# Self attention of a decoder kernel: input scalings over two turns, weights prepared differently, another order on VectorE

## The chip, the cores and the metric

The kernel runs on one core of a Trainium2 chip. A core has five engines that run at the same time, each with its own queue: TensorE (PE) for matmuls and transposes, VectorE (DVE), ScalarE (ACT), GpSimd (POOL), and SyncE (SP), which here only issues DMA transfers. The metric is the device time of one execution in microseconds (us); lower is better. Beside the timed runs there is one profiled execution, from which all durations of single instructions come.

## The reference, cut to what matters

Two decoder layers are computed on x of shape 16 x 112 x 512. The part that the change touches is the first layer's second attention. It has a self part (q, k, v from the normalised x) and a cross part (queries from x, keys and values from a context of 375 rows); the two results go through one output projection together.

```python
def _div_clamp_fp8(x, scale):
    y = jnp.clip(x.astype(jnp.float32) / scale, -FP8_MAX, FP8_MAX)
    return _fp8_roundtrip(y.astype(jnp.bfloat16).astype(jnp.float32))
def _fp8_linear_pertensor(x, wq, w_scale, in_scale):
    xq = _div_clamp_fp8(x, in_scale)
    return jnp.einsum('bsi,oi->bso', xq * in_scale, wq) * w_scale
...
ln_out = _ln(hidden_states, ln_w, ln_b)
q = _ln(_fp8_linear_pertensor(ln_out, wq, wq_scale, q_in_scale).reshape(b, s, g, hpg, d), qln_w, qln_b)
k = _ln(_fp8_linear_pertensor(ln_out, wk, wk_scale, k_in_scale).reshape(b, s, g, d), kln_w, kln_b)
v = _fp8_linear_pertensor(ln_out, wv, wv_scale, v_in_scale).reshape(b, s, g, d)
core = _gqa(q, k, v).reshape(b, s, nh * d)
...
catq = _div_clamp_fp8(jnp.concatenate([core, xout], axis=-1), proj_smooth)
return jnp.einsum('bsi,oi->bso', catq, wproj) * (proj_in_scale * proj_w_scale)
```

So the input is scaled in four ways (for q, k, v and for the cross queries) and rounded to an 8-bit float; the projections are normalised per head; 16 heads share 8 groups of keys; and a scalar, proj_in_scale times proj_w_scale, multiplies the output.

## The kernel before

The program runs in stages; the one concerned is `stage_fp8_self`, from about 286 to 950 us of the profiled span. The 1792 tokens form 14 tiles of 128, the heads four quarters of four. The stage has 64 units of work, each one quarter q and one batch b. Two batches in sixteen (b = 7 and 15) have no tile of their own and do less. The order of units is fixed by `self_order`: eight units of quarter 0, then units of quarters 0 and 1 mixed until unit 24, the rest of quarter 1 to unit 31, quarter 2 from 32 to 47, quarter 3 from 48 to 63.

The loop body is `turn(n)`, which works on several units at once: it projects unit n, computes scores and exponentials of unit n-2, transposes probabilities and multiplies values of unit n-3, transposes queries and keys of unit n-1, and adds the output of unit n-4. The order in which the steps stand in `turn` is the order of instructions on PE and ScalarE for the whole loop, and on VectorE too from turn 5 on (`manual_schedule`). GpSimd's and SP's orders, and VectorE's before turn 5, are set by a planner when the program is built.

What happens in a turn, by engine, with the lines of the profile:

- PE: `ps_q` (L664), scores `ps_s` (L826), transposed probabilities `ps_pt` (L850), `ps_kv` (L664, keys then values), `ps_av` (L858), transposed queries and keys `ps_t` (L819), output `ps_acc` (L664). In some turns also the transposes of an input tile, `ps_xt` (L154). In turns -2 to 4 there are early products for the cross stage, `ps_early` (L653). Weights are in two parts, high and low, so each projection is two products.
- ScalarE: squares of the queries (L761), copy of the probabilities (L852), four exponentials (L839), squares of the keys (L761), copy of the values (L792), queries and keys into batches, `qt` and `kt` (L485).
- VectorE: minimum of the scores, `su_m` (L832), sums of squares, `su_v` (L764), reciprocal (L843), smoothing and rounding of the values (L883, then L504 to L508), normalisation, `qk` (L804), addition to x (L899).
- GpSimd: the last subtraction of a rounding (L510), probabilities times reciprocal (L844), the power of -1/2 for the normalisation (L491 and L492).

The normalisation L804 frees the PSUM banks of `ps_q` and `ps_kv`; there are three banks for the two tiles of each turn.

Three further jobs are woven in. The first is the inputs (`Quantized`). While quarter 0 runs, an input tile is transposed, scaled by 16 ScalarE instructions of one 128x128 block each (L695), rounded on VectorE and GpSimd (`round_qk` for q and k, `round_v` for v; both call `round_fp8`), and written to DRAM for later quarters. Turn n does all of it for unit n+2: the transposes and five scalings around the exponentials, five more and `round_qk` after the key and value products, six more and `round_v` at the end. Inputs come in turns -2 to 4, 6, 8, 10, 13, 15, 17 and 20.

The second is the weights of the next quarter (`Weights`). A piece of 512 columns is loaded in one of two buffers (`begin`), centred on VectorE if it belongs to queries or keys (`centers`: mean L587, L593, subtraction L594), and split into its high part on ScalarE (L617) and its low part on GpSimd (L618) (`ends`). Value and output weights are scaled on ScalarE (L616) ahead of the split. In `turn`, `ends` stands first, `begin` in the middle, `centers` near the end. Quarter 1's weights come two pieces a turn from turn 3, quarter 2's two a turn from turn 24, quarter 3's one a turn from 31, the first cross weights one a turn from 47. The first self weights are prepared in the stage before, the further cross weights in the stage behind, by `step`.

The third is `quantize_cross`: it loads a scaled input tile from DRAM, rounds it for the cross queries and stores it, one of 14 tiles at the end of each turn n in which unit n-4 is of quarter 2 and has a tile.

## Time and profile before

| what | value |
|---|---|
| median of 3 runs | 3885.63 us (3881.12 to 3893.52) |
| the profiled execution, its own time | 3916.36 us |
| its span, first to last instruction | 3914.6 us |
| mean granted TensorE clock | 0.969 |
| PE busy | 3647.7 us (93%) |
| VectorE busy | 1758.7 us (45%) |
| ScalarE busy | 1464.3 us (37%) |
| GpSimd busy | 938.1 us (24%) |

Busy time is a union over an engine's instructions; shares are of the span. The shares are means over seven stages with different limits, so a stage is read by itself. A line of the timeline has the start, the duration, the engine, the line of the program, the operation, output<-inputs and shapes, how many are merged (x8) and, in brackets, how long the engine had been idle and what ended that. "128x512" is partitions by elements. The granted clock is what the throttle gave TensorE[...].

### The profile page before, as it was taken

Reading aid. Unit: us, or ns where it says so; the run is one execution under the profiler, and the core shown is the slowest. Engines: PE = TensorE matmul, PEld = TensorE weight load, DVE = VectorE, ACT = ScalarE, POOL = GpSimd, SP = SyncE. Lnnn points to the kernel's source line nnn. Section 1 sums busy time; section 2 is a strip of 40 time slices with the busy share of each in tenths; the row PEclk is TensorE's granted clock in tenths of the full one; section 3 lists DMA queues with packets and bytes.
Section 4 is the critical chain, followed back from the end, with each engine's and each line's share of the span. In section 5 each row is a group of like instructions: output and inputs, shape, how many; then the busy total and the mean of one; then the engine's idle time right before and its main releaser. Section 6 shows DMA issues by size and latency. Waiting matters only on the chain.

```text
span 3914.6 us, 46312 instructions
## 1 busy us (share of the span) xinstructions
PE 3647.7 (93%) x16482; PEld 2350.9 (60%) x16482; DVE 1758.7 (45%) x3856; ACT 1464.3 (37%) x4189; POOL 938.1 (24%) x1322
## 2 busy tenths in 40 slices
PE   7888788989899999999999999998889989999999
PEld 4445678877556666566666554554344445556788
DVE  4446767775554544544445551111233343214333
ACT  2546666654544444444444430110123341112222
POOL 2333545553322322322222210000222220000000
PEclk8999889999999999999999999999999999999999
DMA  2125323442211211211121115999930013122000
GB/s 74 56 96 171 113 85 117 135 133 75 75 51 60 74 47 48 68 50 51 44 82 48 40 65 180 314 291 260 290 109 12 1 38 111 63 79 81 11 12 17
DMA packets 118117, 364.56 MB, mean 93 GB/s; under 512 B 13280, under 2 KB 33248, under 8 KB 108848
## 3 DMA queue, kind: packets, MB, share of 16 engines
q1 hardware_dynamic: 105504, 332.20, 26.8%
q0 software_dynamic: 5040, 16.52, 1.3%
q10 hardware_dynamic: 7344, 12.89, 1.0%
q8 instruction: 131, 2.15, 0.2%
q14 instruction: 98, 0.80, 0.1%
HBM read 317.09 MB, written 44.47 MB: 92 GB/s over the span
## 4 chain that ended last, share of the span: by engine, by line
PE 68%; DVE 8%; DMA 6%; ACT 3%; POOL 3%; issue 3%; SPq 0%; ACTq 0%; POOLq 0%; DVEq 0%
PE ps_kv L1081 14%; PE ps_acc L664 4%; PE ps L1430 4%; PE ps_q L664 4%; PE ps_av L1134 4%; DMA w_expert<-in_moe_w 3%; PE ps_s L1109 3%; PE ps_u L1785 3%; PE ps_o L341 3%; PE ps_o L1767 3%; PE ps_g L1785 3%; PE ps_q L1536 3%; PE ps_p L1629 3%; PE ps_pt L1124 2%; PE ps_y L1448 2%
## 5 line engine op out<-in xcount | busy, mean ns | idle before, releaser
L1081 PE MATMUL ps_kv<-w_kv,ct 128*125 128x512 f32 x1408 | 637.4, 592 | 0.0
L1081 PEld LDWEIGHTS ps_kv<-w_kv,ct 128*125 128x125 f32 x1408 | 261.1, 187 | 277.2 <-issue 242.1
L1430 PE MATMUL ps<-w_expert,xgt 128*128 128x448 f32 x560 | 222.1, 549 | 19.8 <-DMA w_expert<-in_moe_w 19.1
L510 POOL TENSOR_TENSOR r_o<-r_t,r_m 128x64 fp32r<-128x64 bf16 (+6 forms) x224 | 146.9, 674 | 390.6 <-DVE r_t L508 366.1
L1025 ACT ACTIVATE pr<-ps_s,ex_m 112x375 f32<-112x375 f32 (+1 forms) x272 | 157.7, 580 | 161.6 <-DVE ex_m L1024 151.5
L1057 DVE TENSOR_REDUCE cu_v<-sq 125x2 f32<-125x256 f32 (+1 forms) x248 | 118.5, 478 | 179.3 <-ACT sq L1056 179.0
L233 POOL TENSOR_TENSOR pr<-pr,nq_s 112x448 f32<-112x448 f32 (+1 forms) x120 | 119.5, 996 | 323.7 <-DVE nq_s L232 248.9
L492 POOL TENSOR_TENSOR cu_v<-cu_v,mhalf 125x2 f32<-125x2 f32 (+1 forms) x248 | 190.3, 767 | 20.7
L228 ACT ACTIVATE pr<-ps_s,nq_m 112x112 f32<-112x112 f32 (+1 forms) x480 | 167.7, 374 | 59.0 <-DVE nq_m L220 54.6
L491 POOL TENSOR_SCALAR cu_v<-cu_v 125x2 f32<-125x2 f32 (+1 forms) x248 | 48.2, 194 | 577.9 <-DVE cu_v L1057 575.0
L1109 PE MATMUL ps_s<-kt,qt 128*112 128x375 f32 x512 | 183.0, 479 | 1.3 <-ACT pr L1025 0.9
L1024 DVE TENSOR_REDUCE ex_m<-ps_s 112x1 f32<-112x375 f32 (+1 forms) x272 | 148.4, 545 | 71.8 <-PE ps_s L1656 68.2
L1430 PEld LDWEIGHTS ps<-w_expert,xgt 128*128 128x128 f32 x560 | 104.3, 192 | 117.5 <-issue 107.1
L1056 ACT ACTIVATE sq<-ps_kv 125x256 f32<-125x256 f32 x176 | 67.6, 384 | 273.0 <-PE ps_kv L1081 220.9
L485 ACT ACTIVATE qt<-ps_t,turned 128x448 f32<-128x448 f32 (+6 forms) x224 | 116.6, 582 | 137.6 <-PE ps_t L1093 126.6
L1134 PE MATMUL ps_av<-pt,vn 125*128 125x224 f32 x768 | 161.4, 360 | 0.0
L1124 PEld LDWEIGHTS ps_pt<-ident,pr 112*125 112x125 f32 x768 | 103.5, 190 | 88.6 <-DVE pr L1116 49.9
L242 ACT COPY ptt<-ps_pt 112x448 f32<-112x448 f32 (+1 forms) x120 | 67.4, 561 | 226.3 <-PE ps_pt L240 226.2
L1109 PEld LDWEIGHTS ps_s<-kt,qt 128*112 128x112 f32 x512 | 90.1, 177 | 99.8 <-issue 60.2
L1134 PEld LDWEIGHTS ps_av<-pt,vn 125*128 125x128 f32 x768 | 144.6, 193 | 8.5 <-ACT pt L1127 4.0
L1124 PE MATMUL ps_pt<-ident,pr 112*125 112x112 f32 x768 | 119.0, 286 | 31.5 <-DVE pr L1116 30.5
L485 ACT ACTIVATE kt<-ps_t,vec 128x375 f32<-128x375 f32 (+7 forms) x240 | 131.6, 589 | 26.5 <-PE ps_t L1099 22.3
(294 smaller groups left out, 7426.4 us busy)
## 6 DMA issues: line engine op xcount, KB each, us to landing
w_expert<-in_moe_w SPq DMA_DIRECT2D x105, 896.0 KB
ct<-in_ctx_t SPq DMA_DIRECT2D x64, 750.0 KB
xq<-xq_dram SPq DMA_DIRECT2D x42, 512.0 KB
xq<-xx_dram SPq DMA_DIRECT2D x56, 256.0 KB
raw<-in_self_w SPq DMA_DIRECT2D x48, 256.0 KB
w_sum<-in_ffn_w SPq DMA_DIRECT2D x12, 1024.0 KB
cn<-in_ctx SPq DMA_DIRECT2D x16, 750.0 KB
xv<-xv_dram SPq DMA_DIRECT2D x48, 224.0 KB
```

The lines of the kernel that those rows point to most:

```text
L228: nc.scalar.activation(pr[:, j, :], self.ps[:, j, r * t : (r + 1) * t], AF.Exp, bias=self.mx[r][:, j : j + 1], scale=-1.0, accum_out=sums[ ...
L485: k.nc.scalar.activation(dst, src, AF.Identity, bias=cols[:, 1:2], scale=cols[:, 0:1])
L492: nc.gpsimd.tensor_tensor(dst, dst, bc(k.minus_half[: dst.shape[0]], [dst.shape[0], n]), ALU.pow)
L664: k.nc.tensor.matmul(out, lhs(c), w[i][:, c, :], start=first and c == 0 and i == 0, stop=last and c == n - 1 and i == 1,)
L1024: nc.vector.tensor_reduce(mx, src, AX.X, ALU.min)
L1025: nc.scalar.activation(dst, src, AF.Exp, bias=mx, scale=-1.0, accum_out=sums)
L1081: nc.tensor.matmul(pkv, self.ct[:, c, ch * CC : (ch + 1) * CC], w[:, c, :], start=c == 0, stop=c == KC - 1,)
L1109: nc.tensor.matmul(ps, self.heads.qt[self.b][:, h, :], self.kt[:, h // 2, :], start=True, stop=True)
L1124: nc.tensor.transpose(ps[:, h, :], self.pr[:, h, ch * CC : (ch + 1) * CC], k.ident[:S, :S])
L1134: nc.tensor.matmul(av[:, 2 * g : 2 * g + 2, :], self.vn[:, ch, g, :], self.pt[:, ch, 2 * g : 2 * g + 2, :], start=ch == 0, stop=ch == NCH - 1,
L1430: nc.tensor.matmul(pp, self.xt[:, c, :], w[:, c, :], start=c == 0, stop=c == 3)
L1785: nc.tensor.matmul(pp, w[:, c, cols], xt[:, part, c, :], start=c == 0 and part == 0, stop=c == 3 and part == 1,)
```

## The change

- **Inputs.** Turn n now takes the transposes and the first ten scalings of unit n+2, near its end, and, for unit n+1, `round_qk` behind the query sums, the last six scalings behind the exponentials and `round_v` behind the normalisation.
- **Weights in a turn.** `centers` now treats the pieces loaded in the turn before, behind the minimum, the query sums and `round_qk`; `ends` follows in the same turn behind the exponentials. `centers` also returns whether it centred anything.
- **Output weights.** They are no longer scaled. The scalar `c_proj` is applied when the output is added to x, by one instruction with a scale (L905 in place of L899), in the cross stage too.
- **Value weights.** ScalarE writes the scaled high part at once (two instructions of 256 columns), and the low part is one VectorE instruction for each half (L620: raw times scale less the high part) instead of GpSimd's subtraction.
- **Output of unit n-4.** It comes behind the new input's transposes.
- **Cross roundings.** One tile is taken in every turn from 32 on in which nothing was centred, behind the normalisation, until the 14 are done.

```diff
     def centers(self):
-        for center, end in self.loaded:
-            if center:
-                center()
-            if end:
-                self.begun.append(end)
+        centers = [center for center, _ in self.loaded if center]
+        for center in centers:
+            center()
+        self.begun += [end for _, end in self.loaded if end]
         self.loaded = []
+        return len(centers) > 0
...
         def end():
             hi, lo = self.hi[n][:, cols], self.lo[n][:, cols]
-            if not centered:
-                for i in rows:
-                    part = raw[:, i * width - first : (i + 1) * width - first]
-                    nc.scalar.activation(part, part, AF.Copy, scale=col(i))
-            nc.scalar.copy(hi, raw)
-            nc.gpsimd.tensor_tensor(lo, raw, hi.bitcast(F32), ALU.subtract)
+            if centered or scale is None:
+                nc.scalar.copy(hi, raw)
+                nc.gpsimd.tensor_tensor(lo, raw, hi.bitcast(F32), ALU.subtract)
+                return
+            for i in rows:
+                part = slice(i * width - first, (i + 1) * width - first)
+                nc.scalar.activation(hi[:, part], raw[:, part], AF.Copy, scale=col(i))
+                nc.vector.scalar_tensor_tensor(
+                    lo[:, part], raw[:, part], col(i), hi[:, part].bitcast(F32),
+                    ALU.mult, ALU.subtract,
+                )
...
-    k.nc.vector.tensor_tensor(k.x[:, t, :], k.x[:, t, :], acc, ALU.add)
+    x = k.x[:, t, :]
+    k.nc.vector.scalar_tensor_tensor(x, acc, k.c_proj, x, ALU.mult, ALU.add)
...
         def turn(n):
-            new = inputs.get(n + 2)
-            for w in weights:
-                w.ends()
+            new, half = inputs.get(n + 2), inputs.get(n + 1)
             products(early.get(n, 0))
             if at(n):
                 units[n].project_q(weights[order[n][0]], xq.pop(n))
@@
             if at(n):
                 units[n].query_sums()
-            if new:
-                new.transpose()
+            if half:
+                half.round_qk()
+                xq[n + 1] = half.xq
+            centered = [w.centers() for w in weights]
             if at(n - 3):
                 units[n - 3].transpose_probs()
             if at(n - 2):
                 units[n - 2].exponentials()
-            if new:
-                new.scale(5)
+            for w in weights:
+                w.ends()
+            if half:
+                half.scale(6)
             if at(n):
                 units[n].project_kv(xv[order[n][0]].pop(order[n][1]))
             for w, count, pieces in due(n):
                 w.begin(count, pieces)
-            if new:
-                new.scale(5)
-                new.round_qk()
             if at(n - 3):
                 units[n - 3].values()
             if at(n):
                 units[n].normalize()
+            if half:
+                half.round_v()
+            if n > last[1] and tiles and not any(centered):
+                quantize_cross(k, wk, tiles.pop(0))
             if at(n - 1):
                 units[n - 1].transpose()
-            if at(n - 4):
-                units[n - 4].output()
             if new:
-                new.scale(6)
-                new.round_v()
-                xq[n + 2] = new.xq
+                new.transpose()
+                new.scale(10)
             elif at(n + 2):
                 q, b = order[n + 2]
                 xq[n + 2] = quantized(k, wk, b, xv[q]) if q else None
+            if at(n - 4):
+                units[n - 4].output()
...
-            for w in weights:
-                w.centers()
-            if at(n - 4) and order[n - 4][0] == 2 and units[n - 4].tile is not None:
-                quantize_cross(k, wk, units[n - 4].tile)
```

More of the change, by code (lines that the diff above doesn't have):

```diff
@@ L603, in part @@
         k.raw_load = nc.sync.dma_start(out=raw, in_=src[:, cols])
-        col = lambda i: k.c_proj if scale is None else k.w_cols[:, scale + i : scale + i + 1]
+        col = lambda i: k.w_cols[:, scale + i : scale + i + 1]
         rows = range(first // width, (first + 512) // width)
@@ L954, in due @@
                     yield weights[q + 2], 2 if q == 0 else 1, 3 if n >= last[q] + 4 else 1 + (q < 2)
+        tiles = list(range(TILES))
         def turn(n):
-            new = inputs.get(n + 2)
-            for w in weights:
-                w.ends()
+            new, half = inputs.get(n + 2), inputs.get(n + 1)
             products(early.get(n, 0))
```

## The prediction

> **What bounds the kernel now.** Read first: busy time by stretches. The change sits in the self attention stage (286 to about 950 us of the span): 64 turns, one per pair of quarter and batch, numbered 0 to 63. The first row is turns 5 to 9, then 10 to 24, 25 to 31, 32 to 47, 48 to 63, and last the eight turns 56 to 63 alone.
>
> ```profile
> 389.00:443.60 54.60, 38.59 (x204) 33.09 (x204) 39.82 (x75) 37.62 (x109) 34.05 (x35) 0.81 0.36 121
> 443.60:593.40 149.80, 128.94 (x776) 114.39 (x776) 100.33 (x218) 94.62 (x312) 73.56 (x89) 0.91 0.28 91
> 593.40:657.00 63.60, 55.06 (x352) 48.93 (x350) 46.92 (x104) 41.02 (x126) 38.73 (x42) 0.97 0.39 125
> 657.00:794.00 137.00, 127.54 (x808) 113.10 (x806) 103.55 (x241) 80.87 (x264) 79.01 (x93) 0.96 0.42 137
> 794.00:929.20 135.20, 125.29 (x807) 111.83 (x805) 98.16 (x229) 78.08 (x256) 70.40 (x86) 0.97 0.34 109
> 868.90:929.20 60.30, 60.30 (x406) 54.77 (x403) 39.27 (x92) 37.29 (x124) 29.47 (x38) 1.00 0.28 89
> ```
>
> Columns: stretch, its us, busy PE, PE loads, DVE, ACT, POOL, granted clock, DMA. The last row is the stage undisturbed: PE busy all the time at clock 1.00, 60.3 us for eight turns, 7.54 us each. By that measure turns 5 to 63 need 59 x 7.54 = 444.6 us, and 3.0 for seven input transposes (0.43 each); the distance between the first value products of turns 4 and 63 in the timeline (374.2 and 929.2) is 555. So 107 us of this stage are lost, 2.7% of the kernel. That is all the change can win, but for crumbs elsewhere.
>
> Second, who PE waited for in 316 to 930 us (total, times, longest):
>
> ```profile
> PE ps_av L858 <- ACT pt L852: 27.5, 15, 5.4
> PE ps_kv L664 <- DVE qk L804: 19.3, 10, 4.0
> PE ps_s L826 <- ACT kt L485: 10.1, 7, 3.9
> PE ps_acc L664 <- ACT pr L839: 8.0, 3, 3.0
> ```
>
> These make 65 of some 71 us of idle time; the other 36 of the 107 are matmuls at a reduced clock.
>
> Third, the timeline of one turn with a bad wait (turn 11, kv product at 465.65). VectorE, then PE and ScalarE:
>
> ```profile
> 459.49 0.43 DVE L504 TENSOR_SCALAR y<-y 128x1024 bf16<-128x1024 bf16 x1 [0.90 <-ACT y L695]
> ...
> 460.87 0.69 DVE L508 TENSOR_TENSOR r_t<-y,r_m 128x1024 bf16<-128x1024 bf16 x1
> ...
> 462.13 1.82 DVE L504 TENSOR_SCALAR r_y<-r_y 128x448 bf16<-128x448 bf16 x1
> ...
> 464.92 0.68 DVE L804 TENSOR_TENSOR qk<-ps_q,su_v 128x512 f32<-128x512 f32 x1
> ...
> 467.76 0.62 DVE L832 TENSOR_REDUCE su_m<-ps_s 112x4 f32<-112x448 f32 x1
> ```
> ```profile
> 465.65 1.19 PE L664 MATMUL ps_kv<-w_self,xq 128*128 128x256 f32 x8 [2.68 <-DVE qk L804]
> ```
> ```profile
> 468.47 0.36 ACT L839 ACTIVATE pr<-ps_s,su_m 112x112 f32<-112x112 f32 x1 [3.70 <-DVE su_m L832]
> ```
>
> Ten of the 16 scalings must run on ScalarE before VectorE may round (459.49); the smoothing behind it is held by GpSimd's xq subtraction (1.82 us instead of 0.28); only then comes normalisation, which frees the PSUM bank for which PE waits; and the minimum, whose scores PE had at 462.6, comes at 467.76. Weight turns have the same shape: two centrings stand before the minimum, and the second is stretched:
>
> ```profile
> 599.78 0.75 DVE L594 SCALAR_TENSOR_TENSOR raw<-raw,w_cols,w_mean 128x512 f32<-128x512 f32 x1
> ...
> 601.42 1.68 DVE L594 SCALAR_TENSOR_TENSOR raw<-raw,w_cols,w_mean 128x512 f32<-128x512 f32 x1
> 603.03 0.61 DVE L832 TENSOR_REDUCE su_m<-ps_s 112x4 f32<-112x448 f32 x1
> ```
>
> **The change, part by part.** Step sizes are start-to-start from these timelines. A turn's fixed VectorE work is 5.1 us: minimum 0.54, query sums 0.60, reciprocal 0.15, key sums 0.34, smoothing 1.95, normalisation 0.94, addition to x 0.59. Rounding q and k is 2.0, rounding v 1.3, centring a 512-wide piece 1.65 (two: 3.3), four 256-wide groups 4.5.
>
> *1. Inputs spread (ten scalings at the end of turn n, six in n+1, q/k rounding at the start of n+1).* The count is the same. A turn on ScalarE without scalings is 5.3 us; 16 more at 0.37 make 11.2 against 8.6 of PE, so now one turn overflows and its neighbour idles. Spread: 9.0 and 7.5. Rounding q/k no longer waits for ScalarE in its turn and falls where VectorE waits for the exponentials (1.0 to 1.5 us a turn). Its deadline is one turn nearer: xq is ready about 5 us before its product. The moved DMAs (xq, yx, xv stores) keep their count; on SP the loads queued behind them are wanted two turns later, and the weight load, which waits there for its buffer's last subtraction, now has until the middle of the next turn. The output product moves behind the input's transposes on PE; no engine waits for either at once.
> Turns 5 to 9: VectorE after needs 5.1+3.3+2.0+1.3 = 11.7, then 9.6 (5.1+4.5), 8.4 (no query in turn 7: 3.2, roundings 3.3, two value pieces 1.9), 5.1 and 8.4; with a wait of about 1 us in the long ones, and PE's 8.6 elsewhere, 12.7+10.6+9.4+8.6+8.9 = 50, against 69.3: **-19**. Turns 10 to 24: clean 15 x 7.54 + 2.2 = 115.3; the five turns with roundings are 8.4 of VectorE plus waits, 1.2 above clean each, and 4 for what I do not see: 125 against 149.8: **-25**.
>
> *2. Minimum first, centring behind it, copies after the exponentials.* The exponentials come 3.3 us sooner in two-piece turns. But in the new order the squares of the keys stand on ScalarE behind the weight copies, and those behind the centring of the same turn; GpSimd's order puts a weight subtraction (1.29) ahead of the power for normalisation. Minimum to normalisation then takes about 10 us in two-piece turns against 11.7 (their mean now is 63.6/7 = 9.1 over all kinds). Turns 25 to 31: **-4**. Turns 32 to 63 centre one piece a turn, which fits PE's 8.2; they lose 16.4 and 14.6 now (137.0 and 135.2 less 120.6).
>
> *3. Cross roundings in turns without centring.* Now they meet centrings in turns 48 to 52 (key weights 4.1 us plus rounding 1.4 before the minimum). After, each with its load and its store on SP, ten fall in turns 38 to 47 and four in 53 to 56; VectorE 5.1+1.4 plus waits still fits 8.2, not the short turns of 5.3. With the one-piece centrings of step 2 I count half the 31 us as won: **-15**.
>
> *4. Lighter weights.* Output weights lose their ScalarE scaling (0.73 x 4 a set), value weights a copy and GpSimd's subtraction (2 x 0.62, 2 x 1.29 a set), and VectorE gets four fused subtractions a set. No row shows that form; nearest is the 256-wide L594, 0.48. Floor 0.4, ceiling 0.48 plus a GpSimd xq operation of 2.1 in the way: I take 0.48, so 1.9 a set, counted in turn 7 above. In the first attention and the cross stage (PE busy 1293 of 1330 us) it is behind PE: 0 to -4, take **-1**.
>
> *5. Addition with scale.* The like form is L1802, xo from ps_o with a scalar and x, 128x512: mean 745 ns against 682 for L899. 112 x 0.063 = 7 us of VectorE, mostly under PE; in cross PE waits for VectorE 28.7 us, so at most 3.5 there. Take **+2**, bounds 0 and +7.
>
> *The clock.* [...] Here a wait of 2.74 us (turn 14) is followed by kv matmuls at 2.08 us for eight instead of 1.17; one of 2.68 (turn 11) by 1.19. [...] By the rows nearly all 36 hang on these waits. [...]
>
> Sum: -19 -25 -4 -15 -1 +2 = -62 us. Steps 1 to 3 (63) assume the planned overlap; each engine has its order fixed and each handover (0.2 to 1 us in the waits) delays the next, so I keep three quarters: 63 x 0.75 = 47, less 1 net for 4 and 5: **-46**. The profiled execution took 3916.4 us (span 3914.6) and would take 3870. It is 0.8% above the median of the runs, 3885.6; nothing says that this surplus is in the changed stage, so the same 46 us off the median give **3840 us**.
>
> **Rivals.**
> A, *VectorE stays the bound* (0.15): the work is the same, 5.1 plus up to 6.6 in a turn, and GpSimd's subtractions still stretch two-input operations (0.75 to 1.68 above), now the centring behind the q/k rounding. For it: VectorE busy 39.8 of 54.6 us in turns 5 to 9. Against: half its loss is waits for ScalarE. If only a quarter of steps 1 to 3 is won: 3870.
> B, *all of it is won and the clock stays up* (0.10): 80 to 100 of the 107 us, 3795.
> C, *slower* (0.12): the squares of the keys. They now stand behind six scalings (2.2 us) or the weight copies (1.2, and the centring they wait for), so key sums, power and normalisation come later, and PE's next kv product waits for the bank. From the end of one kv product to the start of the next is 6.3 us; the chain needs 3.0, plus 2.2 fits, plus copies and centring does not. 24 turns have scalings or centring. It decides from 2.6 us of new wait in each, which eats the 62; at 3.4 us, with the half-speed matmuls behind such waits, 82 - 62 = +20: 3905.
> D, *nothing moves* (0.06): another wait of the same length appears (scores for kt, which ScalarE writes last): 3886.
>
> **The numbers.** My case has 0.57 and by itself runs from 3815 to 3862. Within 0.3% (12 us), which is about what a measurement of this kernel tells from no change, is D and a quarter of A (0.04), which runs from 3862 to 3883; the rest of A, my case and B are faster: faster 0.78, same 0.10, slower 0.12. Low is 3802 (B's nearer end), high 3883 (A's far end); C, most of D and the deeper half of B are left out.
>
> **What would show it.** Right: the stretch of the stage shorter by 40 to 60 us, turns 10 to 24 near 8.4 us each, clock there above 0.95, VectorE's waits for ScalarE's y gone, the smoothing near 0.3, PE's waits for qk under 5 us. Wrong: new waits of PE for qk or kt, of VectorE for the key squares, or a centring that waits for its weights' DMA, which is now loaded a turn ahead.

## The result, and the profile after

The changed kernel takes 3876.15 us (median of nine runs, 3872.43 to 3882.13); the kernel before takes 3885.63 in nine runs of its own (3879.88 to 3893.52). The ratio is 0.9978, with a 95% interval of 0.9968 to 0.9988. That is 9.5 us less where 46 were forecast: the sign was right, the size a fifth, and the 0.22% of the ratio lies within the 0.3% that the prediction took for no change.

The profiled execution took 3873.2 us of span against 3914.6, which looks like 41 us; most of it is not the change. The first product of the cross stage stands at 950.9 us of the span before and at 941.7 after, 9.2 us earlier, about the gain of the medians. The other 32 us come after the changed stage. The section on the hardware returns to them.

For the stage, the busy time by stretches of the changed kernel: turns 5 to 9, 10 to 24, 25 to 31, 32 to 47, 48 to 63, and turns 56 to 63 alone. A turn ends where its first value product begins. Columns: stretch, its us, busy PE, PE loads, DVE, ACT, POOL, granted clock, DMA share, GB/s.

```profile
382.30:444.10 61.80, 46.23 (x254) 40.18 (x254) 48.08 (x96) 43.35 (x134) 35.37 (x39) 0.86 0.35 111
444.10:575.50 131.40, 120.40 (x777) 106.21 (x777) 98.83 (x222) 97.55 (x320) 75.33 (x90) 0.99 0.34 113
575.50:640.70 65.20, 56.94 (x352) 50.05 (x350) 50.23 (x103) 37.64 (x120) 33.77 (x38) 0.95 0.37 116
640.70:782.40 141.70, 126.62 (x807) 110.73 (x805) 106.73 (x246) 77.91 (x258) 77.90 (x92) 0.99 0.42 133
782.40:919.90 137.50, 126.60 (x808) 111.97 (x806) 102.17 (x233) 75.78 (x252) 72.23 (x88) 0.98 0.34 109
859.60:919.90 60.30, 59.60 (x385) 53.67 (x385) 43.54 (x98) 34.87 (x115) 31.87 (x40) 0.97 0.31 99
```

The first row that the prediction shows of before (389.00 to 443.60, 54.6 us) leaves out turn 5 and is turns 6 to 9 alone. The prediction's sums use the right 69.3. The row of before to compare with is:

```profile
374.20:443.60 69.40, 47.47 (x251) 40.86 (x250) 47.48 (x95) 47.34 (x140) 40.74 (x43) 0.80 0.36 120
```

Turns 5 to 9 and 10 to 24 became shorter by 7.6 and 18.4 us. Turns 25 to 31 and 32 to 63 became longer, by 1.6 and 7.0. One stretch that the prediction did not sum at all also became longer: from the first early product to the first value product of turn 4 the stage took 87.2 us before and takes 94.7. The balance, -26.0 + 8.6 + 7.5, is -9.9 us.

What PE waits for in 307 to 920 us of the changed kernel (total, times, longest):

```profile
PE ps_s L831 <- ACT kt L485: 17.0, 10, 4.2
PE ps_kv L669 <- DVE qk L809: 11.9, 11, 3.7
PE ps_acc L669 <- ACT pr L844: 9.6, 6, 1.7
PE ps_kv L669 <- POOL xv L510: 8.0, 6, 1.9
PE ps_xt L154 <- ACT y L700: 4.8, 5, 2.2
PE ps_t L824 <- DVE x L905: 4.2, 4, 2.1
...
PE ps_av L863 <- ACT pt L857: 2.1, 3, 1.1
```

The greatest wait of before, 27.5 us for the copied probabilities, has all but gone, and the wait for `qk` fell from 19.3 to 11.9. But `kt` grew from 10.1 to 17.0, and rows that before lacked in this stretch have come: `xv` (8.0), the input's `y` (4.8), the addition to x (4.2).

In the turn that the prediction took apart, the change does what it was to do. VectorE in turn 11 of the changed kernel:

```profile
460.59 0.30 DVE L504 TENSOR_SCALAR r_y<-r_y 128x448 bf16<-128x448 bf16 x1
...
465.19 0.62 DVE L837 TENSOR_REDUCE su_m<-ps_s 112x4 f32<-112x448 f32 x1 [1.31 <-PE ps_s L831]
...
466.35 0.42 DVE L504 TENSOR_SCALAR y<-y 128x1024 bf16<-128x1024 bf16 x1
```

The minimum waits for nothing but its scores, the rounding follows at once without a wait for ScalarE, and the smoothing's first step takes 0.30 us instead of 1.82. Turn 11 took 11.7 us before and takes 8.7. But its neighbours now carry the rest of the same work, and turns 10 to 12 together took 32.3 us before and take 32.4. The gain of 18.4 us lies in turns 14 to 24, above all in 14, 16, 18 and 22. The question is what was lost elsewhere.

### The profile page after: what moved, and what is told of

The parts are those of the page before. It is cut to its first block, busy times and chain, and to the rows that moved or that the text cites. A ratio compares the mean times of both kernels' runs of the same rounds, so it can differ in the third digit from the quotient of the medians.

```text
span 3873.2 us, 46297 instructions
## 1 busy us (share of the span) xinstructions
PE 3631.9 (94%) x16482; PEld 2335.4 (60%) x16482; DVE 1768.5 (46%) x3872; ACT 1438.7 (37%) x4149; POOL 924.6 (24%) x1314
## 5 line engine op out<-in xcount | busy, mean ns | idle before, releaser
L485 ACT ACTIVATE kt<-ps_t,vec 128x375 f32<-128x375 f32 (+7 forms) x240 | 131.5, 589 | 26.9 <-PE ps_t L1105 22.5
```

Source lines behind the costliest of these rows:

```text
L485: k.nc.scalar.activation(dst, src, AF.Identity, bias=cols[:, 1:2], scale=cols[:, 0:1])
```

## The experiments

Every kernel below was timed in five rounds against the kernel before. "The stage" is the time from the first early product to the first cross product of its profiled execution. Where two kernels have the same code in a stretch, it still differs a little: turns 10 to 24 lie between 131.4 and 133.6 us in the changed kernel and three of its variants, turns 48 to 63 are 137.5 and 134.9 in the changed kernel and the first variant. So a difference of 2.6 us in one stretch says nothing. Each stretch comes from one profiled execution; the ratio comes from several runs and is the check.

| kernel | ratio to before, 95% | stage | to turn 4 | 5-9 | 10-24 | 25-31 | 32-47 | 48-63 |
|---|---|---|---|---|---|---|---|---|
| before | 1 | 663.9 | 87.2 | 69.4 | 149.8 | 63.6 | 137.0 | 135.2 |
| changed | 0.9978 [0.9968, 0.9988] | 654.0 | 94.7 | 61.8 | 131.4 | 65.2 | 141.7 | 137.5 |
| scalings first | 0.9952 [0.9941, 0.9963] | 642.8 | 86.5 | 60.1 | 131.5 | 65.8 | 142.2 | 134.9 |
| roundings late | 0.9963 [0.9949, 0.9976] | 652.6 | 94.0 | 62.7 | 133.6 | 65.0 | 139.1 | 136.4 |
| copies behind | 0.9910 [0.9897, 0.9922] | 627.3 | 94.8 | 57.4 | 132.6 | 62.7 | 129.0 | 129.0 |
| roundings as before | 0.9977 [0.9966, 0.9988] | 651.4 | 93.8 | 62.6 | 132.0 | 65.8 | 141.1 | 134.3 |
| both orders | 0.9895 [0.9874, 0.9916] | 620.1 | 87.7 | 56.7 | 131.4 | 62.1 | 130.0 | 130.3 |
| subtractions asked behind | 0.9960 [0.9945, 0.9975] | 650.2 | 94.8 | 61.8 | 131.3 | 65.7 | 139.9 | 134.9 |
| inputs alone | 0.9944 [0.9923, 0.9965] | 639.8 | 95.1 | 59.7 | 129.8 | 64.2 | 134.5 | 134.8 |
| arithmetic alone | 1.0031 [1.0017, 1.0045] | 674.1 | 89.6 | 73.9 | 148.6 | 64.3 | 139.2 | 136.7 |
| subtractions behind | 0.9939 [0.9918, 0.9960] | 638.7 | 94.1 | 62.9 | 131.4 | 65.3 | 131.3 | 131.9 |
| both, old arithmetic | 0.9866 [0.9846, 0.9886] | 614.7 | 86.5 | 55.9 | 131.4 | 63.8 | 127.4 | 128.1 |
| both, roundings away | 0.9869 [0.9850, 0.9887] | 612.9 | 86.1 | 56.9 | 131.5 | 62.1 | 126.0 | 127.6 |
| all four | 0.9861 [0.9842, 0.9880] | 612.4 | 88.1 | 55.9 | 131.6 | 63.7 | 124.2 | 126.4 |

The stage's change explains the ratio in every row to within 4 us (both orders: 43.8 us off the stage, 41 by the ratio times 3887).

### Scalings first, in turns -2 to 4

```diff
+            if half and n < 5:
+                half.scale(6)
             products(early.get(n, 0))
...
-            if half:
+            if half and not (n < 5):
                 half.scale(6)
```

> The changed kernel, but in turns -2 to 4 the last six scalings of an input stand first in the turn on ScalarE, ahead of the squares of the queries, instead of behind the exponentials. Theory (one PSUM bank for the transposed input is held through the early products and the exponentials, so the next input's transposes wait, and PE cools): from the first early product to the first value product of turn 4 the stage takes 94.7 us in the changed kernel and 87.2 in the one before; here 87 to 90, and the time 5 to 8 us below the changed kernel's 3876, a ratio to before of about 0.996. Rival (the prologue is limited by what ScalarE and VectorE have to do in all, or the squares of the queries, now behind six scalings, are late instead): the stretch stays at 93 to 97 and the ratio at 0.9975 or above.

The stretch to turn 4 fell to 86.5 us, below the kernel before, and the time by 0.26% of before against the changed kernel: the theory holds. The timeline of the changed kernel shows how it lost these 8 us (PE and ScalarE, turn 2 into turn 3):

```profile
348.92 0.60 ACT L766 ACTIVATE sq<-ps_q 128x512 f32<-128x512 f32 x1 [7.27 <-PE ps_q L669]
...
352.13 2.21 ACT L700 ACTIVATE y<-ps_xt,q_bias,q_gain 128x128 bf16<-128x128 f32 x6
...
354.40 0.66 PE L154 MATMUL ps_xt<-ident,xn 128*128 128x128 f32 x4 [2.20 <-ACT y L700]
354.89 8.73 PE L658 MATMUL ps_early<-w_kv,w_ct 128*125 128x512 f32 x16
```

There is one PSUM bank for a transposed input (`tr=1` where the stage is set up). It is free once all 16 scalings have read it. In the changed order the last six stand behind the squares and the exponentials of the next turn. ScalarE, in order, sits idle for 7.27 us during PE's early products with six scalings ready behind the squares that it waits for. Then it does them at 352.13, and PE, which has finished everything else, waits 2.20 us for the bank. The 16 early products behind that wait take 8.73 us: the granted clock is half from 355.28 to 358.70. In the variant the same place reads:

```profile
349.24 0.60 PE L154 MATMUL ps_xt<-ident,xn 128*128 128x128 f32 x4
349.68 7.03 PE L658 MATMUL ps_early<-w_kv,w_ct 128*125 128x512 f32 x16
```

No wait, full clock, and 7.03 us for the same products. The difference of 1.70 us is half of the 3.41 us that the clock stood at half. In the whole stretch to turn 4 it stood there for 10.2 us in the changed kernel and 3.4 here, and PE idles for 7.9 us there and 3.4 here. Half of the first difference and the whole of the second make the 8 us.

### Cross roundings behind the output of unit n-4

```diff
-            if n > last[1] and tiles and not any(centered):
-                quantize_cross(k, wk, tiles.pop(0))
             if at(n - 1):
                 units[n - 1].transpose()
...
                 units[n - 4].output()
+            if n > last[1] and tiles and not any(centered):
+                quantize_cross(k, wk, tiles.pop(0))
```

> The changed kernel, but the rounding of a cross input stands behind the output of unit n-4, at the end of the turn, in the same free turns. Theory (the rounding delays the addition to x, which frees a PSUM bank for the scores, and PE waits in ps_t for it): turns 32 to 63 take 279.2 us in the changed kernel and 272.2 before; here 270 to 275, and the ratio to before falls from 0.9978 to about 0.9965. Rival 1 (it is the next minimum that the rounding delays, wherever it stands between two minima): turns 32 to 63 stay within 2 us of 279. Rival 2 (the free turns themselves are wrong, since they are those that start a run of centrings): no change here, but one in the kernel with the roundings in their old turns.

Turns 32 to 63 took 275.5 us, 3.7 less than in the changed kernel, at the theory's weak end, and the two intervals overlap. The place within the turn is not where most of the loss is.

### Weight copies and subtractions behind the key squares

```diff
-            for w in weights:
-                w.ends()
             if half:
                 half.scale(6)
             if at(n):
                 units[n].project_kv(xv[order[n][0]].pop(order[n][1]))
+            for w in weights:
+                w.ends()
             for w, count, pieces in due(n):
```

> The changed kernel, but the copies and subtractions of the new weights stand behind the squares of the keys and the copy of the values, instead of ahead of them. Theory (rival C of the prediction: the squares of the keys stand on ScalarE behind weight copies that wait for the centring, so key sums, power and normalisation come late): turns 5 to 9 fall from 61.8 us to 57 to 60, turns 25 to 31 from 65.2 to 60 to 63, VectorE's waits of su_v for ScalarE's squares from 33.9 us to under 27, and the ratio to before to about 0.996. Rival (the copies come too late for the buffers of the next load, or VectorE's own work is what is long): no stretch changes by more than 1.5 us, or the loads of weights are waited for.

Two lines moved by two places take 26.7 us off the stage: 4.4 in turns 5 to 9, 2.5 in 25 to 31, and 21.2 in 32 to 63, for which nothing had been expected. VectorE's waits for ScalarE's squares over the stage went from 43.1 to 22.9 us. To see the mechanism, take the same turn (34 into 35, one piece centred) in both kernels. First the changed one, all engines in time:

```profile
672.05 0.62 ACT L614 CAST w_self<-raw 128x512 fp32r<-128x512 f32 x1 [0.73 <-DVE raw L594]
...
672.58 0.38 ACT L766 ACTIVATE sq<-ps_kv 128x256 f32<-128x256 f32 x1
...
672.99 0.42 DVE L769 TENSOR_REDUCE su_v<-sq 128x2 f32<-128x256 f32 x1 [0.88 <-ACT sq L766]
...
673.14 1.28 POOL L615 TENSOR_TENSOR w_self<-raw,w_self 128x512 fp32r<-128x512 f32 x1
...
674.70 1.34 POOL L492 TENSOR_TENSOR su_v<-su_v,mhalf 128x6 f32<-128x6 f32 x1
...
676.08 0.69 DVE L809 TENSOR_TENSOR qk<-ps_q,su_v 128x512 f32<-128x512 f32 x1 [0.47 <-POOL su_v L492]
...
677.68 0.62 DVE L837 TENSOR_REDUCE su_m<-ps_s 112x4 f32<-112x448 f32 x1
```

The copy waits for the centring (0.73), the squares stand behind the copy, the key sums wait for the squares (0.88), and GpSimd makes the weight's low part (1.28 us) ahead of the power. So VectorE is late with the normalisation and comes to the next minimum at 677.68 without a wait. VectorE has become the chain: turn 35 takes 8.51 us where PE needs 8.17. The variant:

```profile
661.35 0.38 ACT L766 ACTIVATE sq<-ps_kv 128x256 f32<-128x256 f32 x1
...
661.96 0.39 DVE L769 TENSOR_REDUCE su_v<-sq 128x2 f32<-128x256 f32 x1
661.99 0.62 ACT L614 CAST w_self<-raw 128x512 fp32r<-128x512 f32 x1
...
663.40 1.34 POOL L492 TENSOR_TENSOR su_v<-su_v,mhalf 128x6 f32<-128x6 f32 x1
...
664.72 1.29 POOL L615 TENSOR_TENSOR w_self<-raw,w_self 128x512 fp32r<-128x512 f32 x1
...
667.27 0.62 DVE L837 TENSOR_REDUCE su_m<-ps_s 112x4 f32<-112x448 f32 x1 [0.81 <-PE ps_s L831]
```

The squares come first, the key sums wait for nothing, the power stands ahead of the low part, and the minimum has to wait 0.81 us for PE: PE is the chain again, at 8.17 to 8.19 us a turn. A third of a microsecond a turn is the smaller part of the 21.2 us, and only ten or so of these 32 turns centre a piece. Turns 37 and 53, which come at the end of such runs of turns, lost 2.2 us each, and turns 32, 48 and 56, each behind a short turn, 4.0, 2.1 and 2.8: together 13.3. In each of the last three the clock was at half for 3.41 us in the changed kernel (some 1.7 us lost, half of it, an estimate), and in none of turns 32 to 63 in this variant.

### Cross roundings where the kernel before has them

```diff
-            if n > last[1] and tiles and not any(centered):
-                quantize_cross(k, wk, tiles.pop(0))
...
+            if at(n - 4) and order[n - 4][0] == 2 and units[n - 4].tile is not None:
+                quantize_cross(k, wk, units[n - 4].tile)
```

> The changed kernel, but the cross inputs are rounded where the kernel before rounds them: at the end of turns 36 to 51, whatever else stands there. Theory (the move into free turns is what costs turns 38 to 47 and 53 to 58 their 7 us): turns 32 to 63 fall from 279.2 us to 265 to 272, since the one-piece centrings keep their gain. Rival (the old places collide with the centrings of turns 48 to 52, as the prediction held): 279 to 287.

275.4 us in turns 32 to 63 against 279.2, between what the two cases said, and the ratio is that of the changed kernel: neither the loss nor a gain of step 3 lies in which turns were chosen, as long as the weight copies stand where they do.

### Both orders

```diff
+            if half and n < 5:
+                half.scale(6)
             products(early.get(n, 0))
...
-            for w in weights:
-                w.ends()
-            if half:
+            if half and not (n < 5):
                 half.scale(6)
             if at(n):
                 units[n].project_kv(xv[order[n][0]].pop(order[n][1]))
+            for w in weights:
+                w.ends()
```

> The changed kernel with both orders altered: the six scalings first in turns -2 to 4, and the new weights' copies and subtractions behind the squares of the keys. Theory (two separate orders cost the change what the prediction had counted): alone they took 11.2 and 26.7 us off the stage of 654.0, so together 614 to 619 us from the first early product to the first cross product, some 46 us under the kernel before, and a ratio to before of 0.986 to 0.990, which is the forecast of 3840. Rival (a third wait takes over once both are gone): 622 us or more, ratio 0.991 or above.

The stage is at 620.1 us, 43.8 under the kernel before, and the ratio is 0.9895, or 41 us. The ratio is in the range of the theory, the stage 1 us above it: the two stage gains (11.2 and 26.7) add to within 4 us. What PE still waits for in this kernel (300 to 886 us):

```profile
PE ps_kv L669 <- POOL xv L510: 9.8, 7, 3.1
PE ps_s L831 <- DVE r_m L506: 7.2, 2, 4.0
PE ps_acc L669 <- ACT pr L844: 6.7, 4, 1.7
PE ps_s L831 <- ACT kt L485: 6.5, 4, 4.3
...
PE ps_kv L669 <- DVE qk L809: 2.7, 4, 1.2
```

`qk` is down to 2.7 from 19.3 before, `kt` to 6.5 from 10.1.

### Which engine's order: ScalarE's copy or GpSimd's subtraction

```diff
-                w.ends()
+                w.copies()
...
             if at(n):
                 units[n].project_kv(xv[order[n][0]].pop(order[n][1]))
+            for w in weights:
+                w.rests()
```

> The changed kernel, but only the subtractions of the new weights (GpSimd's, and VectorE's for value weights) stand behind the squares of the keys; ScalarE's copies stay ahead of them. With all of it behind, the stage went from 654.0 to 627.3 us. If it is ScalarE's order that costs (rival C as the prediction had it: the squares wait behind copies that wait for the centring), the stage stays at 648 to 655. If it is GpSimd's order (a weight subtraction of 1.29 us ahead of the power for the normalisation), it falls to 627 to 634. In between: both.

The run did not do what it was for. GpSimd's order is planned, and its planner put the subtraction in front again:

```profile
654.10 1.29 POOL L628 TENSOR_TENSOR w_self<-raw,w_self 128x512 fp32r<-128x512 f32 x1
655.36 0.23 POOL L491 TENSOR_SCALAR su_v<-su_v 128x6 f32<-128x6 f32 x1
```

On GpSimd and ScalarE nothing moved; on VectorE only the key sums of two turns, 29 and 39, now stand ahead of the low part of the value weights. Turns 32 to 63 took 274.8 us, 4.4 less than in the changed kernel, but 3.4 of that lie in turns 32 and 48, in which the order is the same. So the same kernel was run with GpSimd's order written out:

```diff
-        with k.tc.manual_schedule(engines=fixed | {mybir.EngineType.DVE}):
+        with k.tc.manual_schedule(engines=fixed | {mybir.EngineType.DVE, mybir.EngineType.Pool}):
```

> The changed kernel, with ScalarE's copies of new weights where they are (ahead of the squares of the keys), but GpSimd's subtractions now really behind the power for the normalisation: GpSimd's order is written out from turn 5 on, which the run before this one lacked, so that its planner kept the subtraction in front. If GpSimd's 1.29 us ahead of the power is what costs turns 32 to 63 their 21 us (279.2 in the changed kernel, 258.0 with everything behind), they fall to 258 to 264. If it is ScalarE's copies ahead of the key squares (rival C in the prediction's words), they stay at 274 to 280.

```profile
650.46 1.32 POOL L492 TENSOR_TENSOR su_v<-su_v,mhalf 128x6 f32<-128x6 f32 x1
651.74 1.43 POOL L628 TENSOR_TENSOR w_self<-raw,w_self 128x512 fp32r<-128x512 f32 x1
```

Now the power is first, and turns 32 to 63 fall to 263.2 us, within the 258 to 264 expected of it. Of the 21.2 us that the copies cost there, 16.0 are gone with ScalarE's copy left where it was, 11.6 of them with GpSimd's order. The remaining 5.2 (263.2 to 258.0) are not shown to be ScalarE's copy: they are as much as three stretches of half clock may cost (10.2 us at half, of which half, some 5 us, is lost by estimate), which this kernel has in turns 40, 48 and 56. The kernel with both orders, whose copies are behind, has three as well and takes 260.3. In turns 5 to 9 and 25 to 31 it is the other way round: 127.0 us in the changed kernel, 127.5 and 128.2 in these two, 120.1 with the copies behind; there it is ScalarE's copy. Writing out GpSimd's order also moved a few loads on SP and some other work on GpSimd, which this comparison includes.

### The inputs alone

This is the kernel before with the input lines of the change and nothing else of it:

```diff
-            new = inputs.get(n + 2)
+            new, half = inputs.get(n + 2), inputs.get(n + 1)
...
+            if half:
+                half.round_qk()
...
+                half.scale(6)
...
+                half.round_v()
...
+                new.transpose()
+                new.scale(10)
```

> The kernel before with the input part alone: scalings and roundings spread over two turns, weights, cross roundings and the addition as before. The prediction's step 1 said 44 us less in turns 5 to 24 (219.2 us before), three quarters of it kept: 33. The changed kernel has 26.0 less there and 7.5 more in the prologue. Theory (step 1 is right in turns 5 to 24, but has the prologue's cost in it): prologue 93 to 96 us, turns 5 to 24 at 185 to 198, turns 25 to 63 as before, ratio 0.994 to 0.998. Rival (the gain of turns 5 to 24 comes from the order on VectorE, step 2): turns 5 to 24 at 205 or more, ratio 0.999 or above.

The input part is worth 24.1 us of the stage and 0.56% of the time, as the theory had it. Turns 5 to 24 take 189.5 us, 29.7 less (33 was forecast), and the prologue is 7.9 longer. One part of the change alone gained more than twice what the whole did; the other parts, as they stood, gave 14 us back.

### The arithmetic alone

This is the kernel before with the new `end()` of the weights and the scaled addition, as in the diff of the change.

```diff
+            if centered or scale is None:
+                nc.scalar.copy(hi, raw)
+                nc.gpsimd.tensor_tensor(lo, raw, hi.bitcast(F32), ALU.subtract)
+                return
...
+    k.nc.vector.scalar_tensor_tensor(x, acc, k.c_proj, x, ALU.mult, ALU.add)
```

> The kernel before with the arithmetic of the change alone: output weights unscaled, value weights' scale and low part on ScalarE and VectorE, the scalar in the addition to x. The prediction's steps 4 and 5: -1 and +2, so +1 us (bounds -4 and +7): ratio 0.999 to 1.002, turns 5 to 63 within 3 us of 555. Rival (lighter ScalarE and GpSimd work is worth more than counted, since key squares and powers stand behind it): ratio 0.997 or below, with turns 25 to 63 shorter by 5 us or more.

It is slower: 12 us by the ratio, 10.2 in the stage, most of it in turns 5 to 9 (4.5) and 32 to 63 (3.7). The rows of VectorE in the stage:

```profile
L905 DVE SCALAR_TENSOR_TENSOR x<-ps_acc,c_proj,x 128x512 f32<-128x512 f32 x52 | 38.6, 742 | 5.2 <-PE ps_acc L669 5.2
L620 DVE SCALAR_TENSOR_TENSOR w_self<-raw,w_cols,w_self 128x256 fp32r<-128x256 f32 x12 | 7.7, 695 | 0.0
```

The addition is as expected (742 ns against 678 in the stage of before). The low part takes 695 ns in the mean, not 480: nine of the twelve take 0.47 to 0.52 us, and three that overlap a subtraction on GpSimd 1.25 to 1.38. These two rows are some 11 us more of VectorE's time. But the stage does not lose them evenly: turns 8, 28 and 40 became 2.3 to 3.0 us longer, turn 27 became 3.1 shorter, and in turns 5 to 63 the clock is at half for 92.2 us instead of 75.1, which is some 6 of the 10 us (an estimate, half of PE's busy time in it). Relieving ScalarE and GpSimd bought nothing that shows.

### Both orders, with the arithmetic of before

```diff
-            if centered or scale is None:
+            if not centered:
...
+                    nc.scalar.activation(part, part, AF.Copy, scale=col(i))
+            nc.scalar.copy(hi, raw)
+            nc.gpsimd.tensor_tensor(lo, raw, hi.bitcast(F32), ALU.subtract)
...
-    k.nc.vector.scalar_tensor_tensor(x, acc, k.c_proj, x, ALU.mult, ALU.add)
+    k.nc.vector.tensor_tensor(k.x[:, t, :], k.x[:, t, :], acc, ALU.add)
```

> The kernel with both orders altered (stage 620.1 us), but with the arithmetic of the kernel before: output weights scaled on ScalarE, value weights with scaling, copy and GpSimd's subtraction, plain addition to x. In the kernel before the lighter arithmetic alone cost 10 us of the stage. If this is the 63 ns more per addition and VectorE's share of the value weights, it costs as much here: stage 609 to 614. If it was only where waits happened to fall in the old order (turns 8, 28, 40, 48 moved by 2 to 3 us each, the rest hardly), the stage is at 617 to 626.

The stage falls by 5.4 us to 614.7 and the median from 3843.8 to 3838.9; the intervals overlap. That is just above the range of the first case and half of what the arithmetic cost in the old order. It is not spread over the turns as 63 ns an addition would be: 6.9 us come off turns 42, 48 and 56, and others became longer. In these three turns the kernel with both orders has the clock at half for 3.41 us each; here it is never at half in turns 32 to 63. So the size is uncertain, and the cause is at least in part the second case, where the waits happened to fall.

### Both orders, no cross rounding in or behind a short turn

```diff
-            if n > last[1] and tiles and not any(centered):
+            if n > last[1] and tiles and not any(centered) and units[n].tile is not None and units[n - 1].tile is not None:
```

> The kernel with both orders altered, but no cross rounding in the two short turns without a tile (39, 47, 55) nor in the turn behind each (40, 48, 56). Theory (the 1.4 us rounding does not fit a turn of 5.3 us, the next minimum and the addition to x come late, and turns 40, 42, 48 and 56, which take 11.0, 12.6, 12.3 and 12.6 us, lose 2.8 to 4.4 each): turns 32 to 63 fall from 260.3 us to 248 to 254, the ratio to before from 0.9895 to about 0.987. Rival (what is displaced makes the next turns late instead): 258 to 263.

Turns 32 to 63 fall to 253.6 us, the slow end of what was expected. Turn 42 is clean now (8.2 us instead of 12.6). Turns 40, 48 and 56 still take 11.0, 10.7 and 11.2, so the rounding is only part of their trouble. About 5 of the 6.7 us that turns 32 to 63 gain (an estimate, half of 10.2 us) are the same three stretches of half clock, which are gone here too. The variant with the copies behind alone has the same code in these turns as both orders, and none of these stretches; it takes 258.0 us, and against it the gain is 4.4. So the same code ran in these turns with 10.2 us at half clock in one profile and with none in another. How a short turn hurts shows best in the changed kernel, turns 55 and 56 (VectorE, PE and ScalarE):

```profile
855.45 0.29 DVE L504 TENSOR_SCALAR r_y<-r_y 128x512 bf16<-128x512 bf16 x1 [0.56 <-DMA r_y<-yx_dram]
...
856.78 0.74 DVE L905 SCALAR_TENSOR_TENSOR x<-ps_acc,c_proj,x 128x512 f32<-128x512 f32 x1
857.44 0.61 DVE L837 TENSOR_REDUCE su_m<-ps_s 112x4 f32<-112x448 f32 x1
857.58 0.44 PE L824 MATMUL ps_t<-ident,qk 128*128 128x128 f32 x2 [2.08 <-DVE x L905]
858.15 0.35 ACT L844 ACTIVATE pr<-ps_s,su_m 112x112 f32<-112x112 f32 x1 [4.21 <-POOL xqx L510]
...
859.70 3.11 PE L669 MATMUL ps_acc<-w_self,r_o 128*128 128x512 f32 x8 [1.68 <-ACT pr L844]
```

The rounding and its wait for the DMA stand ahead of the addition to x. PE waits 2.08 us for the PSUM bank that the addition frees. The minimum comes last, the exponentials after it (the row names `xqx`, which ended within 0.05 us of the minimum), and the output product waits another 1.68 us for the bank of their scores; it then takes 3.11 us instead of 2.08, since the clock is at half from 860.46 on.

### All four edits

The two orders, the old arithmetic, and the cross roundings away from short turns and late in the others, in one kernel:

```diff
+            if half and n < 5:
+                half.scale(6)
...
-            for w in weights:
-                w.ends()
...
+            for w in weights:
+                w.ends()
...
                 units[n - 4].output()
+            if n > last[1] and tiles and not any(centered) and units[n].tile is not None and units[n - 1].tile is not None:
+                quantize_cross(k, wk, tiles.pop(0))
...
-    k.nc.vector.scalar_tensor_tensor(x, acc, k.c_proj, x, ALU.mult, ALU.add)
+    k.nc.vector.tensor_tensor(k.x[:, t, :], k.x[:, t, :], acc, ALU.add)
```

> All four edits that took time off, in one kernel: scalings first in turns -2 to 4, weight copies and subtractions behind the key squares, no cross rounding in or behind a short turn and the others behind the output of unit n-4, and the arithmetic of the kernel before. From the stage of 620.1 us with the first two, the arithmetic took 5.4 and the roundings' turns 7.2; if these add, and the place at the turn's end takes another 1, the stage is at 605 to 609 us and the ratio to before at 0.984 to 0.986. Rival (the arithmetic and the roundings take the same waits away, in turns 40 to 48 and 56): 610 to 614, ratio as in the two runs before, 0.987.

This has the lowest median of all, 3832.1 us (ratio 0.9861). But the rival was right: the stage is at 612.4 us, no shorter than with the roundings away alone, since the prologue came out 2 us longer and the gains of turns 32 to 63 overlap in part (9.7 us off both orders' 260.3, where the two edits alone took 4.8 and 6.7). Against those two kernels the interval does not tell it apart.

## Why the prediction was wrong, step by step

**What bounds the kernel** was read rightly: 107 us lost in turns 5 to 63. The best variants brought some 50 of them in.

**Step 1, turns 5 to 9 (-19) and 10 to 24 (-25).** Right in kind, and with the three quarters kept nearly right in size: 29.7 us with the inputs alone against 33. Turns 10 to 24 gained 18.4, against 18.8 with the same factor. Turns 5 to 9 gained 7.6 where 14 remain of the 19 with that factor, and 12.0 with the copies behind: most of what is missing there belongs to step 2. The deadline ("xq is ready about 5 us before its product") did not hold: the changed kernel waits 3.2 us for `xq` and 8.0 us for `xv` in its products, 6.0 of the latter in turns 10 to 19, where no piece is centred.

**Step 1, the prologue.** This step failed by absence: turns -2 to 4 got no term, that is nothing, without a reason. They hold seven of the fourteen inputs, and there the last six scalings were moved behind a wait of ScalarE's while the only PSUM bank for transposes stayed taken. Cost: 7.5 us in the changed kernel, 7.9 with the inputs alone, gone when the scalings go first.

**Step 2 and rival C.** Here the prediction failed most, by 27 of its 36 missing us. Step 2 named both facts, the key squares behind the copies and GpSimd's subtraction ahead of the power, and then priced them only for turns with two centrings. Of turns 32 to 63 it said that they "centre one piece a turn, which fits PE's 8.2", which counts VectorE's work and not the handovers in its chain: with waits of 0.88 and 0.47 us a one-piece turn took 8.51, and VectorE was late in the short turns too: 31, 39 and 55 took 0.7 to 0.9 us longer than with the copies behind. Rival C had the mechanism, but as a threshold ("from 2.6 us of new wait in each"), in PE's chain, and as all or nothing. PE's waits for `qk` and `xv` in the kv products came to 19.9 us, under 1 us for each of its 24 turns, far from the threshold, and the order cost 26.7 us all the same. It also looked at ScalarE alone, where in turns 32 to 63 GpSimd's order cost about 11.6 and a cost of ScalarE's copy is not shown.

**Its own signs.** Of the signs of being right, the clock in turns 10 to 24 (0.99) and the smoothing (0.30 us) came; PE's waits for `qk` stayed at 11.9 us, not under 5. The signs of being wrong came too: PE's waits for `kt` grew from 10.1 to 17.0 us, and VectorE's for the squares from 29.6 to 43.1.

**Step 3 (-15).** Turns 32 to 63 became 7.0 us longer. With the copies behind they are 14.2 shorter than before, so the 15 were there, but behind the order above. The cross roundings' new turns contributed nothing that can be measured in the changed kernel, and with both orders repaired they still cost 4.4 to 6.7 us for lying in and behind short turns. "Not the short turns of 5.3" was said, and no price was put on it.

**Steps 4 and 5 (-1, +2).** Together +1 was forecast with bounds from -4 to +7; alone they measured +10 in the stage, outside the bounds, and about +5 in the repaired order, both in good part through the clock. The addition's 63 ns were right (742 against 678). So was the low part's own time, 0.47 to 0.49 us where 0.48 was taken. But the case that the prediction named as its ceiling is there: in the changed kernel five of the twelve overlap an operation on GpSimd and take 1.14 to 2.22 us, and the mean is 842 ns; with the copies behind it is 512. What the sum left out is the clock: in turns 42, 48 and 56 of the kernel with both orders it stood at half for 3.41 us each, and with the arithmetic of before it never did in turns 32 to 63.

**The clock.** The prediction put nearly all of the 36 us at a reduced clock down to waits such as the one of 2.74 us in turn 14. What PE was busy above its floor of 447.6 us (444.6 and the 3.0 for the transposes) fell from 36.7 us before to 29.2 in the changed kernel and 17.9 with the copies behind. The traces list the granted clock: in turns 5 to 63 it was at half for 75.1, 37.5 and 20.5 us in these three kernels, in 13, 9 and 4 stretches. At half clock the early products start 853 ns apart, at full clock 429. With half of PE's busy time in the stretches counted as lost (an estimate from these distances), that is 31, 17 and 9 us, so the clock is most of the 36 us of before, as the prediction took it. The other 6 to 12 us above the floor are not traced.

Which waits did it is less plain: turn 11 has a wait of 2.68 us, and the eight kv matmuls behind it took 1.19 us, where turn 14's took 2.08. In the traces of before and of the changed kernel, the stretches at half clock in turns 5 to 63 are 3.41, 6.83 or 13.65 us long, and they begin and end whole steps of 3.41 us apart. Cut into such steps, the profile reads as follows (columns as above): the end of the wait in turn 11 of before, turn 14 of before, and turn 56 of the changed kernel.

```profile
463.80:467.21 3.41, 1.56 (x13) 1.56 (x14) 3.24 (x10) 0.97 (x3) 1.06 (x2) 1.00 0.49 192
```
```profile
487.70:491.10 3.40, 1.42 (x12) 1.21 (x12) 3.30 (x5) 3.40 (x11) 2.12 (x2) 1.00 0.02 5
491.11:494.52 3.41, 1.14 (x5) 1.14 (x6) 3.24 (x9) 1.39 (x4) 1.62 (x3) 0.50 0.61 212
```
```profile
857.05:860.45 3.40, 1.19 (x5) 0.87 (x6) 1.79 (x5) 2.30 (x11) 1.54 (x2) 1.00 0.34 114
860.46:863.86 3.40, 3.40 (x9) 2.63 (x8) 3.12 (x6) 1.54 (x4) 2.07 (x3) 0.50 0.03 6
```

In turn 14, a wait of 2.13 us and the start of the one of 2.74 lie in the same step: PE is busy for 1.42 of its 3.40 us, and the clock is 0.50 in the next. In turn 56 two waits of 2.08 and 1.68 us lie in one step, with PE busy for 1.19 us, and the clock is 0.50 behind it. Turn 11's wait of 2.68 us is divided between two steps, in which PE is busy for 2.22 and 1.56 us, and the clock stays at 1.00. In turns 5 to 63 of these two traces the clock falls 22 times. In the step ahead of each fall PE was busy for 4% to 49% of the time; in the steps at full clock that no fall followed, for 46% or more. The clock came back behind steps with PE busy for 85% or more, and stayed at half behind those with 82% or less. So the length of a single wait did not tell the cases apart here: the two waits of turn 56 were shorter than turn 11's.

**Median and profile.** The forecast did not credit the 31 us by which the profiled execution of before exceeded its median to the stage. That was right.

**The three quarters.** In the kernel with both orders the stage gained 43.8 us, close to the 46. That doesn't confirm the factor of three quarters: it was one guess for everything that the sum did not follow, and the largest of what it did not follow, the order on GpSimd and ScalarE, has been taken out there. Rival B's nearer end, 80 us, would be 3806 and not 3802; nothing hangs on it.

## What to carry to other kernels

When an order is changed, price every instruction that now stands behind a wait, on each engine in turn, the planned ones too, and in every kind of turn; an order that made seven full turns late by 0.3 us each also cost 2 to 4 us in each of five others, and 26.7 us of the 46 forecast in all. Count handovers in the chain of the engine that is nearly full, not its busy time alone. A stretch in which a change moves instructions gets a term in the sum even if nothing is wrong there now. And before a difference of some 5 us between two profiles is put down to an edit, compare how long the clock stood at half in each: in turns 32 to 63 two kernels with the same code there had 10.2 us of it and none.

## What the runs showed of the hardware

PE lost speed after short waits: the output product behind two waits of 2.08 and 1.68 us took 3.11 us instead of 2.08, and the 16 early products behind one wait of 2.20 us took 8.73 instead of 7.03. Both times the granted clock was at half for 3.41 us, behind a step of 3.41 us in which PE had been busy for 1.19 and 1.21 us.

The mixture-of-experts stage, in which nothing was changed, waited for its weights in some executions and not in others. Its rows in the kernel before, and in the one with both orders and the old arithmetic:

```profile
PE ps L1430 <- DMA w_expert<-in_moe_w: 19.1, 15, 2.5
```
```profile
PE ps L1432 <- DMA w_expert<-in_moe_w: 11.6, 20, 1.4
```

The changed kernel and ten of the twelve variants had no such row; the roundings late had one of 10.1 us. The span outside the changed stage was 3250.7 us before, 3234.3 in the second of these, and 3219.2 in the changed kernel. Of the 31.5 us between the first and the last, 19.1 are this wait, and some 11 (an estimate, half of 22) the clock, which behind the stage stood at half for 125 us before and 103 after. So the difference of two profiled spans told four times the gain of the medians, and only the distance between two products of the stage told the change's own.
